# ScalarE in place of VectorE for the absolute values of ten FP4 weight blocks, with other delays in the order of a decoder kernel

## The chip, the core and the metric

The kernel runs on one core of one Trainium2 chip. The metric is the device time of one execution, in microseconds (us). The engines are called as in the profile: PE (TensorE matmuls), PEld (TensorE weight loads), DVE (VectorE), ACT (ScalarE), POOL (GpSimd) and SP (SyncE, which here only issues DMAs).

## The reference

The input is 16 sequences of 128 tokens with 256 features, a context of the same shape and an integer mask. Two layers follow each other, each of self-attention, cross-attention and a feed-forward part, each part followed by a residual sum and a layer norm:

- layer 0 attention: 16 heads, queries and keys projected to 32 latent features with a rotary table, causal softmax;
- layer 0 cross-attention: linear attention with the context (`q (k^T v)`), an affine layer norm;
- layer 0 feed-forward: a gated unit of 704 hidden features, whose three weights and two activations are rounded to FP4;
- layer 1 attention: causal softmax and a second, linear term (`leaky_relu`, `sigmoid`);
- layer 1 cross-attention: masked softmax, and within it a feed-forward part of 1024 hidden features;
- layer 1 feed-forward: one linear map, weights and activations rounded to FP6.

The part that the change touches is this rounding, along the last dimension in blocks of 16:

```python
scale = jnp.maximum(jnp.max(jnp.abs(xb), axis=-1, keepdims=True) / 6.0, 1e-12)
xn = xb / scale
idx = jnp.searchsorted(_MID, jnp.abs(xn))
q = _GRID[idx] * jnp.sign(xn) * scale
```

with the grid 0, 0.5, 1, 1.5, 2, 3, 4, 6 and the midpoints between its values. Everything is float32.

## The kernel before

**Work and stages.** A tile is one sequence: 128 tokens on the partitions. `stages(b, s)` is the work of sequence `b` from the first projection to the output DMA. It is a Python generator, as are its parts (`l0_attn`, `l0_xattn`, `l0_ffn`, `l1_attn`, `l1_xattn`, `l1_ffn`) and the helpers in them. Eight sequences are in flight, each in a place of its own in SBUF (`place0` to `place7`, tags `A`, `B`, `C`, `D`, `x`, `v` with the number of the place); when one ends, another starts in its place. Sequences 0 to 7 are the first wave, 8 to 15 the second.

**The order.** Nothing is scheduled by the compiler. A generator yields what its next step needs: an engine, buffers, tiles that must have been written. A class `Clock` keeps at build time an estimate of when each engine is free and when each tile is written; `Run.start()` gives from it the time at which a step could begin. The loop at the end of `decoder_kernel` looks at all generators, takes those that could begin within 0.05 us of the earliest, and among them first one that holds an open tile, then the one whose time of readiness plus a delay, rounded to steps of 2 us, is the earliest. The delays are the 17 numbers of `DELAY`: one for each sequence (the weights share the first) and one for `fold_values`, which prepares layer 0's value weights. That step's instructions are then issued on their engines; each engine runs its own instructions in the order of issue, waiting on semaphores. So one changed estimate or delay moves what comes after on all engines. Nearly all instructions bear line 208, which is the recording helper's.

**Fillers.** `Timed.fill` (line 147) is called before each step that begins on PE. Where the estimate has PE idle for at least `LEAST` us, it issues small bf16 matmuls into a spare PSUM bank (`ps_filler`, line 161) for 75% of the gap. They compute nothing that is used.

**Weights.** `quantised_weights` is a generator like the others. It takes `w_gate` and `w_up` in three blocks each of 128x512 (in buffers that the profile calls `raw_e`, `raw_A`, `raw_B` for the gate and `raw_C`, `raw_D`, `raw_t` for the other), and `w_down` in four of 128x384 or 128x320 (`raw_down`); rounds each with `fp4`; transposes it on PE (`ps_wt_...`) and copies it with ACT to `gu` and `down`. The first wave's feed-forward (`ps_pg`, `ps_pu`, then `ps_tr_hq` and, after a copy `hT`, `ps_dn`) waits for these. The buffers that hold the raw blocks lie in the eighth place, which sequence 7 takes when the weights are done.

**Rounding.** `to_grid` makes on DVE the block maximum `am`, the scale `sc` and its reciprocal `rc`; the product with `rc`; then the step of the grid at each value from its absolute value, in `st` (tiles `fc_...`); then rounds by adding and subtracting it, and multiplies with `sc`. The absolute value has two ways in FP4, by the parameter `by_act`, which is False in all calls:

```python
        elif by_act:
            yield "S", xn, sc, st
            S.activation(st, xn, AF.Abs)
            yield "V", st, xn, sc
        else:
            yield "V", xn, sc, st
            V.tensor_scalar(st.bitcast(U32), xn.bitcast(U32), 0x7FFFFFFF, None, ALU.bitwise_and)
```

In the second way the pass over the bits stands on DVE; FP6 (`low is None`) uses ACT already.

**Attention.** Scores are written to one PSUM tile of four banks, `quad`, of which there is one: scores `ps_s`, row maxima on DVE (`nm`), their three bf16 terms on POOL (`maxima`), a transpose `ps_tm`, the scores again transposed `ps_st` with the maxima subtracted, exponentials on ACT (`e`), for causal attention a select on POOL, products with the values `ps_yp`, a copy `ys`, transposes `ps_ty`, the division on DVE. Names that end in `_a` are the self-attentions, in `_x` the cross-attention of layer 1. `ps_lat` is the latent projection of layer 0 (with `rope` on DVE).

Of the kernel before, what the change touches and what calls it, by code (L numbers as in the profile page):

```python
# [15 lines left out]
B, T, D, H, HD, LAT = 16, 128, 256, 16, 16, 32  # L16
# [5 lines left out]
NFC = 6  # L22
HID = 1024
EPS = 1e-5
SHARE, LEAST = 0.75, 1.4

DELAY = (0.04, 0.26, 0.15, 0.27, 0.15, 0.52, 0.34, 0.45, 0.56, 0.30, 0.28, 0.08, 0.47, 0.04, 0.22, 0.10, 0.51)
WINDOW = 3.413


# [183 lines left out]
def decoder_kernel(ctx: ExitStack, tc: tile.TileContext, a: dict, out: bass.AP):  # L214
# [31 lines left out]
    def mine(s, tag, shape, name, dtype=F32):  # L246

        return ring(own, f"{tag}{s}", 1, shape, dtype, name)
# [34 lines left out]
    def arrives(t):  # L283
        clock.wrote[clock.key(t)] = ("Q", max(clock.free["PE"], clock.free["Q"]) + 2.5)
# [19 lines left out]
    for g in range(4):  # L304
        n = 512 if g < 3 else NB
# [62 lines left out]
    for i in range(0, 5, 2):  # L368
        n = min(2, 5 - i)
# [68 lines left out]
    def bank(shape, name, dtype=F32):  # L438
        return psum(ps_p, "p", shape, name, dtype)

    def work(tag, bufs, shape, name, dtype=F32):
        return ring(wk, tag, bufs, shape, dtype, name)
# [24 lines left out]
    g, c, n = place["a1p"]  # L467
# [47 lines left out]
    def transposed(src, n_chunks, dst, name):  # L515

        yield "PE", "p", src
        t = bank((n_chunks, P), f"tr_{name}")
        for i in range(n_chunks):
            PE.transpose(t[:, i, :], src[:, i * P : (i + 1) * P], ident)  # L520
        yield "S", t
        S.copy(dst, t)
# [171 lines left out]
    def to_grid(dst, src, n, size, top, least, magic, low, name, by_act=False):  # L694

        width = n * size  # L700
        lock = "fC" if width > D else "fc"
        yield "V", lock, src
        st = work(lock, 1, [P, width], f"fc_{name}")
        s3 = src.rearrange("p (n s) -> p n s", s=size)
        am, sc, rc = (ring(sm, k + lock, 1, [P, n], F32, f"{k}_{name}") for k in ("am", "sc", "rc"))
        V.tensor_reduce(am, s3, AX.X, ALU.max, apply_absolute_value=True)
        V.tensor_scalar(sc, am, 1.0 / top, least, ALU.mult, ALU.max)
        V.reciprocal(rc, sc)
        if low is not None:
            V.tensor_scalar(rc, rc, low, None, ALU.mult)  # L710
        yield "V", rc, sc, st
        xn = dst
        x3 = xn.rearrange("p (n s) -> p n s", s=size)
        V.tensor_tensor(x3, s3, rc.unsqueeze(2).to_broadcast([P, n, size]), ALU.mult)
        if low is None:

            yield "S", xn, st, sc
            S.activation(st, xn, AF.Abs)
            yield "V", st, sc
            V.scalar_tensor_tensor(xn, st, -(2.0**-23), xn, ALU.mult, ALU.add)  # L720
# [7 lines that stand above are left out]
        V.tensor_scalar(st, st, 1.5, magic, ALU.max, ALU.mult)  # L728
        yield "V", xn, st, sc
        V.tensor_tensor(xn, xn, st, ALU.add)  # L730
        V.tensor_tensor(xn, xn, st, ALU.subtract)
        yield "V", xn, sc, st
        V.tensor_tensor(
            dst.rearrange("p (n s) -> p n s", s=size), x3, sc.unsqueeze(2).to_broadcast([P, n, size]), ALU.mult
        )

    def fp4(dst, src, width, name, by_act=False):

        yield from to_grid(dst, src, width // 16, 16, 6.0, 1e-12, 2.0**22, 1.0 - 2.0**-23, name, by_act)

    def fp6(dst, src, width, name):

        yield from to_grid(dst, src, width // 32, 32, 7.5, 1e-30, 2.0**20, None, name)
# [185 lines left out]
    def quantised_weights():  # L929
        yield ("V",)  # L930
        GP.memset(down[:64, NFC - 1, :], 0.0)
        downs = []
        for which, name in enumerate(("w_gate", "w_up")):
            for t, i, j in raws[name]:
                q = t[:, i : i + 2, :].rearrange("p j d -> p (j d)")
                yield from fp4(q, q, 2 * D, f"{name}_{j}")
                yield "PE", "p"
                p = bank((4, P), f"wt_{name}_{j}")
                for jj in range(2):
                    for kc in range(2):  # L940
                        PE.transpose(p[:, 2 * kc + jj, :], q[:, jj * D + kc * P : jj * D + (kc + 1) * P], ident)
                n = min(2 * P, FF - j * P)
                clock.kept.discard(clock.key(t))
                yield "S", p
                for kc in range(2):
                    S.copy(
                        gu[:, which, kc, j * P : j * P + n],
                        p[:, 2 * kc : 2 * kc + 2, :].rearrange("p j n -> p (j n)")[:, :n],
                    )
            for at, n in ((0, 384), (384, 320)):  # L950
                q = mine(NS - 1, "ABCD"[len(downs)], [P, n], f"raw_down_{which}_{at}")
                nc.sync.dma_start(out=q, in_=a["w_down"][:, which, at : at + n])
                downs.append((which, at // P, n, q))
        for j, f0, n, q in downs:
            yield from fp4(q, q, n, f"down_{j}_{f0}")
            yield "PE", "p"
            t = bank((3, P), f"wt_down_{j}_{f0}")
            for f in range(3):
                at = min(f * P, n - P)
                PE.transpose(t[:, f, :], q[:, at : at + P], ident)  # L960
            yield "S", t
            if f0 == 0:
                S.copy(down[:, 0:3, j * P : (j + 1) * P], t)
            else:
                S.copy(down[:, 3:5, j * P : (j + 1) * P], t[:, 0:2, :])
                S.copy(down[64:, 5, j * P : (j + 1) * P], t[64:, 2, :])
        release("gu", [gu, down])
        release("place", [gu])
        for j in range(2):
            yield "V", "t2"  # L970
            q = work("t2", 3, [P, D], f"raw_f1_{j}")
            nc.sync.dma_start(out=q, in_=a["w_f1"][:, j, :])
            arrives(q)
            yield "V", q
            yield from fp6(q, q, D, f"wf1_{j}")
            yield from transposed(q, 2, wf[:, :, j * P : (j + 1) * P], f"wf1_{j}")
# [221 lines left out]
    def release(name, tiles):  # L1198
        if name == "place":
            name = f"place{NS - 1}"  # L1200
        at = max(clock.done(t) for t in tiles)
        free[name].extend([at] * (B if name in ("gu", "wv", "bt") else 1))
# [47 lines left out]
    for name in ("w_x1v", "w_x1o", "w_1", "w_2"):  # L1250
        load(name, nc.sync)
    runs = [
        Run(-1, NS, fold_values(), ("PE",)), Run(0.7, NS, later_biases(), ("PE",)),
        Run(0.5, NS, quantised_weights(), ("V",)),
    ]
    opened.clear()
# [17 lines left out]
    while runs:  # L1274
        able = [(r.start(), r.age, r) for r in runs]
        able = [r for r in able if r[0] is not None]
        first = min(r[0] for r in able)


        at, _, run = min(  # L1280
            (r for r in able if r[0] <= first + 0.05),
            key=lambda r: (not r[2].held, round((r[2].ready + DELAY[int(r[1]) if r[1] >= 0 else B]) / 2.0), r[1]),
        )
        run.step(at)
        if run.need is None:
            runs.remove(run)
# [116 lines left out]
```

## Time and profile before

| | us |
|---|---|
| median of 3 runs | 964.27 |
| lowest, highest | 961.06, 965.34 |
| profiled execution | 960.91 |
| its span, first to last instruction | 959.2 |

| engine | busy, us | share of the span |
|---|---|---|
| PE | 891.0 | 93% |
| DVE | 701.0 | 73% |
| ACT | 515.7 | 54% |
| POOL | 432.5 | 45% |

DMA moves 25.6 MB, mostly in the first 72 us. PE's clock is granted at 0.99 of full speed in the mean. A line of a group reads: line, engine, operation, output and inputs, shapes, count, then busy us and mean ns of one, then the idle time of the engine just before these instructions and what ended it. A wait reads: engine and tile that waited, engine and tile that it waited for, us in total, times, longest. Matmuls overlap in the array, so the means of single matmuls add up to more than PE's busy time.

### The profile page before, as it was taken

What the parts mean: (1) busy time and instruction counts of PE and PEld (TensorE: products, weight loads), DVE (VectorE), ACT (ScalarE), POOL (GpSimd) and SP (SyncE); (2) the same over time, 40 slices, a digit from 0 to 9 for tenths busy, and PEclk for the clock granted to TensorE, in tenths of its full rate; (3) what the DMA queues carried; (4) which work ended last, traced back from release to release, by engine and by line L of the source; (5) the groups of instructions that cost most, each with busy time, mean ns of one, the idle gap of its engine ahead of it and who ended that gap; (6) DMA issues with size and microseconds to landing.
All of it is one profiled execution on the core that took longest, in us unless ns stands there. A gap on an engine that the chain in (4) does not pass through costs nothing.

```text
span 959.2 us, 28184 instructions
## 1 busy us (share of the span) xinstructions
PE 891.0 (93%) x11882; PEld 711.3 (74%) x11882; DVE 701.0 (73%) x1440; ACT 515.7 (54%) x1119; POOL 432.5 (45%) x898
## 2 busy tenths in 40 slices
PE   6788999899999999999999999998999999999985
PEld 6575666676878788878887776776777878877863
DVE  5899999778975945554768788759858687654564
ACT  3254374475577555555455456546765664654532
POOL 3325444465444446343444454554435353453332
PEclk9999999999999999999999999999999999999998
DMA  7920100000000000010000000000000000100000
GB/s 232 207 71 7 29 13 2 15 10 10 11 23 5 12 27 20 18 30 13 13 15 27 23 25 23 13 13 11 15 10 7 16 6 2 37 5 24 2 12 11
DMA packets 47863, 25.55 MB, mean 27 GB/s; under 512 B 23005, under 2 KB 45517, under 8 KB 47481
## 3 DMA queue, kind: packets, MB, share of 16 engines
q1 hardware_dynamic: 46816, 22.39, 8.6%
q8 instruction: 93, 1.52, 0.6%
q0 software_dynamic: 192, 0.93, 0.4%
q10 hardware_dynamic: 728, 0.44, 0.2%
q14 instruction: 34, 0.27, 0.1%
HBM read 19.57 MB, written 2.10 MB: 23 GB/s over the span
## 4 chain that ended last, share of the span: by engine, by line
PE 53%; DVE 30%; ACT 6%; POOL 6%; issue 4%; POOLq 0%; ACTq 0%; DVEq 0%
PE ps_ff L208 10%; PE ps_s_a L208 3%; DVE nm_a L208 3%; PE ps_st_a L208 3%; DVE rope L208 3%; PE ps_a1qk L208 2%; DVE hh L208 2%; PE ps_st_x L208 2%; PE ps_qk L208 2%; PE ps_dn L208 2%; PE ps_pg L208 2%; PE ps_yt L208 2%; PE ps_pu L208 2%; PE ps_yp_a L208 2%; PE ps_s_x L208 2%
## 5 line engine op out<-in xcount | busy, mean ns | idle before, releaser
L208 POOL TENSOR_SCALAR_AFFINE_SELECT e_a<-e_a 128x1024 f32<-128x1024 f32 x64 | 78.4, 1227 | 75.4 <-ACT e_a L208 75.2
L208 DVE TENSOR_REDUCE nm_a<-ps_s_a 128x16 f32<-128x2048 f32 x32 | 73.1, 2283 | 17.3 <-PE ps_s_a L208 17.2
L208 ACT ACTIVATE e_a<-ps_st_a 128x1024 f32<-128x1024 f32 x64 | 65.7, 1032 | 17.7 <-PE ps_st_a L208 17.5
L208 ACT ACT_TABLE_LOAD x47 | 60.3, 1283 | 12.7 <-DMA brow<-in_rows_dram 8.8
L208 PE MATMUL ps_ff<-yT_x1t,w 128*128 128x128 f32 x512 | 62.9, 276 | 0.5 <-ACT yT_x1t L208 0.5
L208 PEld LDWEIGHTS ps_ff<-yT_x1t,w 128*128 128x128 f32 x512 | 60.1, 192 | 2.4 <-issue 0.9
L208 PE MATMUL ps_ff<-w,ff 128*128 128x256 f32 x256 | 61.3, 383 | 0.0
L208 PEld LDWEIGHTS ps_ff<-w,ff 128*128 128x128 f32 x256 | 46.3, 190 | 7.6 <-issue 1.8
L208 ACT ACTIVATE ff<-ps_ff,cols 128x128 f32<-128x128 f32 x128 | 36.6, 370 | 27.4 <-PE ps_ff L208 27.0
L208 POOL CAST maxima<-nm_a 128x16 bf16<-128x16 f32 x32 | 9.8, 307 | 89.1 <-DVE nm_a L208 89.1
L208 PE MATMUL ps_dn<-qw_down,hT 128*128 128x256 f32 x192 | 47.5, 384 | 1.1 <-ACT yT_x1t L208 1.1
L208 DVE TENSOR_REDUCE nm_x<-ps_s_x 128x16 f32<-128x2048 f32 x16 | 36.5, 2282 | 11.4 <-PE ps_s_x L208 11.4
L208 PE MATMUL ps_pg<-gu,yT_xq 128*128 128x352 f32 x128 | 44.1, 467 | 0.1
L208 PE MATMUL ps_pu<-gu,yT_xq 128*128 128x352 f32 x128 | 43.1, 459 | 0.0
L208 ACT ACTIVATE x_x<-z_x,rstd_x 128x256 f32<-128x256 f32 x32 | 19.2, 601 | 42.5 <-POOL rstd_x L208 39.2
L208 PEld LDWEIGHTS ps_dn<-qw_down,hT 128*128 128x128 f32 x192 | 34.6, 190 | 8.0 <-issue 2.1
L208 ACT ACTIVATE e_x<-ps_st_x 128x1024 f32<-128x1024 f32 x32 | 31.5, 1023 | 15.7 <-PE ps_st_x L208 15.7
L208 ACT ACTIVATE x_a<-h_a,rstd_a 128x256 f32<-128x256 f32 x32 | 19.3, 603 | 31.8 <-POOL rstd_a L208 30.6
L208 PE MATMUL ps_yp_a<-e_a,v_a 128*32 128x128 f32 x1024 | 35.3, 276 | 1.1 <-POOL e_a L208 1.1
L208 POOL TENSOR_TENSOR rot<-rope,rope 128x512 f32<-128x512 f32 x16 | 21.3, 1330 | 29.6 <-DVE rope L208 27.8
L208 PEld LDWEIGHTS ps_pu<-gu,yT_xq 128*128 128x128 f32 x128 | 24.3, 190 | 13.5
L208 POOL TENSOR_TENSOR x1k<-x1k,mb 128x512 f32<-128x512 f32 x16 | 21.8, 1365 | 27.2 <-ACT x1k L208 27.2
(367 smaller groups left out, 2638.0 us busy)
## 6 DMA issues: line engine op xcount, KB each, us to landing
ctx<-in_ctxT_dram SPq DMA_DIRECT2D x32, 128.0 KB
xT_in<-in_xT_dram SPq DMA_DIRECT2D x16, 128.0 KB
w<-in_w_dram SPq DMA_DIRECT2D x2, 1024.0 KB
x_in<-in_x_dram SPq DMA_DIRECT2D x16, 128.0 KB
out_dram<-out SPq DMA_DIRECT2D x16, 128.0 KB
a1qa<-x_f SPq DMA_DIRECT2D x16, 127.0 KB
mi<-in_mask_dram SPq DMA_DIRECT2D x16, 64.0 KB
rows<-in_rows_dram POOLq DMA_DIRECT2D x1, 768.0 KB, 5.7
```

The lines of the kernel that those rows point to most:

```text
L208: return f(*args, **kw)
```

## The change

The FP4 rounding of the ten weight blocks takes its absolute values with an ACT activation (`AF.Abs`) in place of DVE's pass over the bits; the rounding of activations stays as it was. The 17 delays are others, `LEAST` goes from 1.4 to 1.2 us, and the loop takes only entries that could begin at the earliest time, where it allowed 0.05 us more.

```diff
-SHARE, LEAST = 0.75, 1.4
+SHARE, LEAST = 0.75, 1.2
-DELAY = (0.04, 0.26, 0.15, 0.27, 0.15, 0.52, 0.34, 0.45, 0.56, 0.30, 0.28, 0.08, 0.47, 0.04, 0.22, 0.10, 0.51)
+DELAY = (0.04, 0.25, 0.07, 0.45, 0.31, 0.03, 0.03, 0.44, 0.09, 0.44, 0.38, 0.30, 0.51, 0.36, 0.34, 0.24, 0.46)
...
-                yield from fp4(q, q, 2 * D, f"{name}_{j}")
+                yield from fp4(q, q, 2 * D, f"{name}_{j}", True)
...
-            yield from fp4(q, q, n, f"down_{j}_{f0}")
+            yield from fp4(q, q, n, f"down_{j}_{f0}", True)
...
-            (r for r in able if r[0] <= first + 0.05),
+            (r for r in able if r[0] <= first + 0.0),
```

## The prediction

> **What bounds the kernel now.** I read the page first: the busy shares and the forty slices.
>
> ```profile
> span 959.2 us, 28184 instructions
> PE 891.0 (93%) x11882; PEld 711.3 (74%) x11882; DVE 701.0 (73%) x1440; ACT 515.7 (54%) x1119; POOL 432.5 (45%) x898
> ...
> PE   6788999899999999999999999998999999999985
> ...
> DVE  5899999778975945554768788759858687654564
> ...
> PEclk9999999999999999999999999999999999999998
> ...
> PE 53%; DVE 30%; ACT 6%; POOL 6%; issue 4%; POOLq 0%; ACTq 0%; DVEq 0%
> ```
>
> One slice is 24 us. PE is full from slice 7 on. In slices 2 to 6 it is DVE that is full, and PE is not. The last line is the chain that ended last: ACT holds 6% of it. The busy time of each engine in three stretches (after the length: PE, PEld, DVE, ACT, POOL; near the end the granted clock) says the same in numbers:
>
> ```profile
> 24.00:144.00 120.00, 103.62 (x1496) 73.35 (x1496) 114.27 (x212) 53.49 (x110) 50.66 (x82) 0.98 0.28 65
> 144.00:912.00 768.00, 739.12 (x9970) 598.34 (x9972) 546.91 (x1119) 438.75 (x948) 358.22 (x747) 1.00 0.05 15
> 912.00:959.00 47.00, 33.04 (x271) 24.84 (x263) 25.95 (x71) 15.27 (x38) 13.99 (x36) 0.94 0.04 12
> ```
>
> From 24 to 144 DVE is busy 114.3 of 120 us, while PE has 16.4 us free and spends 11 of its 103.6 on filler. From 144 to 912 PE is idle 28.9 of 768 us. In the last 47 us it is idle 14. So an edit can save DVE time at the beginning, PE idle time spread thinly over the middle, or idle time in the tail. The chain at 39 to 46 us shows the removed pass on the path:
>
> ```profile
> 39.49 0.61 DVE raw_B L208
> ...
> 40.13 1.43 DVE fc_w_gate L208
> ...
> 41.58 0.44 DVE fc_w_gate L208
> ...
> 43.46 2.21 DVE nm_a L208
> ```
>
> **Removed and added passes.** DVE loses ten passes over the bits. The groups by form give them: four of 0.427, 0.417, 0.426 and 0.428 and one more of 0.427 us, one of 1.421 (raw_B, while GpSimd ran a tensor_tensor), two of 0.338 and two of 0.588: 5.40 us in all. ACT gains ten Abs. No 128x512 Abs is in the trace; bounds are the 128x256 Abs of fp6 and the 128x512 Identity with a pointer bias:
>
> ```profile
> L208 ACT ACTIVATE fc_f<-f1q 128x256 f32<-128x256 f32 x16 | 6.7, 417 | 1.9 <-DVE f1q L208 1.9
> ...
> L208 ACT ACTIVATE q<-ps_qfk,wqk_b 128x512 f32<-128x512 f32 x16 | 11.1, 692 | 4.2 <-PE ps_qfk L208 4.1 <-DMA w_x1o<-in_w_x1o_dram 0.2
> L208 DVE TENSOR_SCALAR fc_w_gate<-raw_B 128x512 uint32<-128x512 uint32 x1 | 1.4, 1421 | 0.0
> ```
>
> I take 0.61 us, from 0.417 plus 256 elements at 0.73 ns (the slope from the 0.370 us of a 128x128 ACTIVATE to the 1.023 of a 128x1024 one), and 0.51 for 384 columns. That adds some 5.8 us to ACT, which has more than half of 24 to 144 free. What matters is whether DVE waits for the answer. The built order of the changed kernel shows what stands between the product and the next pass on DVE. For six blocks there is other work: raw_A (the l2o sum, and its wait for PE), raw_C (a 2.28 us maximum), raw_t (0.67 us) and three of the four down blocks (over 1 us each). There the pass is saved whole: 0.417 + 0.426 + 0.427 + 0.588 + 0.338 + 0.588 = 2.78 us. For four blocks nothing stands between, and DVE waits for Abs with 0.05 us of hand-over: raw_e 0.66 for 0.427, +0.23; raw_B 0.66 for 1.421, -0.76; raw_D 0.66 for 0.428 and about 0.5 behind an exponential that ACT has queued ahead, +0.73; the first down block 0.56 for 0.338, +0.22. Sum: -2.78 + 0.42 = **-2.4 us** on a stretch that DVE bounds. Bounds: -5.4 (no wait shows) to +4: Abs stands in ACT's order behind an exponential once and once behind the copy of ys, which itself waits for PE; that copy's chain (exponential 1.03, select 1.23, products 1.0, copy 0.59) is 3.9 us if none of it is done. Behind the waiting DVE pass are rope and the score maxima, for which PE waits.
>
> The Trainium skill speaks against this move: "ScalarE: Activation LUTs", section "Rules for kernel authors", sends simple elementwise operations to VectorE and not to ScalarE. The rows agree on the durations (0.396 us on DVE against 0.417 on ACT at 256 columns, both SBUF to SBUF); by the rule alone the term would be a small loss, ten times 0.02, and the sum below -2.7 in place of -5.3. The rule does not ask which engine is full, and from 24 to 144 us it is DVE.
>
> **The order.** The delays, the choice among ready entries (0.05 us became 0.0) and LEAST reorder everything. Four things can be read from the built order.
>
> Table loads fall from 47 to 35, as silu and exponentials alternate less often; no Abs brings one. ACT's timeline shows a load's price:
>
> ```profile
> 203.49 1.28 ACT L208 ACT_TABLE_LOAD   x1
> 204.78 0.47 ACT L208 ACTIVATE silu<-ps_pg 128x352 f32<-128x352 f32 x1
> 205.27 1.28 ACT L208 ACT_TABLE_LOAD   x1
> 206.56 1.02 ACT L208 ACTIVATE e_a<-ps_st_a 128x1024 f32<-128x1024 f32 x1
> ```
>
> So 12 x 1.283 = 15.4 us less on ACT. ACT has 6% of the chain: **-0.9 us**, bounds 0 to -15.4. "ScalarE: Activation LUTs", section "What ACT_TABLE_LOAD costs", adds a drain of about 1.38 us to each load, which would make 12 x 2.66 = 31.9 and -1.9 on the path; here a load begins 0.02 us after the instruction before it and the next begins 0.01 after it, so no drain is seen.
>
> The tail. From the end of the last masked scores (918.5) to the first feed-forward product of batch 15 (933.7) pass 15.2 us, in which PE has 11.5 us of work by its own rows. Waits of PE from 912 on:
>
> ```profile
> PE ps_tr_f L208 <- DVE f1q L208: 2.9, 2, 1.9
> PE ps_tr_x1t L208 <- DVE x L208: 2.7, 2, 1.6
> PE ps_tr_x1y L208 <- DVE y_x L208: 1.0, 1, 1.0
> ```
>
> In the changed order three batches end together: 17.8 us of PE work stand in that place, enough to cover the chain of batch 15, and one more output projection (1.2 us) has moved behind its last product, into time in which PE only fills. I take **-4 us**: the 3.7 idle, the 1.2, less about 1 for a new planned gap ahead of batch 14. Bounds -7 to +1.
>
> Fillers go from 99 to 111 (47 to 66 before the first down product, 16 to 7 in the middle, 36 to 38 at the end). At 23.0 us for 99 that is 2.8 us, and 4.4 for the 19 at the beginning. They are set where PE is planned idle, and DVE covers them: **0**, bounds 0 to +4.4.
>
> The down product. It needs the copy of the transposed activations (0.35 to 0.62 us on ACT). In the old order at least 1.8 us of PE work stands between in 15 of 16 batches. In the new one eight have 0.3, 0.4, 0.4, 0.5, 0.9, 1.1, 1.2 and 1.3. With a copy that starts at once (0.7 us) they lack 1.2 us together; with the shortest time that the old trace shows (1.73) 7.7. I take **+2**.
>
> The rest of the order is the unknown. By 48 us slices PE's time without work varied by about 1.7 us from slice to slice in the middle, so 16 slices of another order differ by some 7, and two orders by 10: **0**, bounds -10 to +10.
>
> Sum: -2.4 - 0.9 - 4 + 0 + 2 = -5.3 us. The profiled execution took 960.91 (span 959.2 and 1.7 around it), 3.4 under the median of the runs; on it the sum gives 955.6, and on the median of 964.27 it gives **959.0**. About 0.5%, 4.8 us, is what a measurement here can tell from no change, so the forecast lies just beyond it. Its own range is 950 to 963.
>
> **Rivals.** One: the order takes back what the edit and the tail give (chance 0.25). For it: PE's planned gaps, by the fillers, are about as long as before, and the middle has only 28.9 us of idle to win. Then the time is 964, between 959.5 and 969.
>
> Two, slower (0.32): the copies for the down product come late. Place: eight down products between about 145 and 600 us. If the copy finds ACT in a pair of exponentials (2 x 1.03), each lacks 0.7 + 2.06 us less its cover, together 8 x 2.76 - 6.1 = 16 us in place of the 2 counted: -7.3 + 16 = +8.7, 973 us. It decides from 12.1 us, 1.5 for each product. Against it: ACT is free 45% of the time, and loses 12 loads.
>
> That the change does not do what it says is ruled out by the built order: ten DVE passes are gone, ten Abs are on ACT, nothing else in the counts but loads and fillers differs.
>
> **The numbers.** Faster (0.43) holds the forecast and larger gains, for which the bounds of loads and order leave room to 945. The low end, 946, takes in the order's -10 on the forecast; the high end, 975, takes in rival two.
>
> **What would show it.** Right: DVE busy near 109 of 24 to 144 and the first down product earlier than 145.7 us; no wait of PE for the last batch's x over 1 us; 35 loads. Wrong: DVE idle on fc for over 4 us in all; PE waiting for yT or hT before ps_dn by over 5 us; PE idle over 35 us from 144 to 912.

## The result and the profile after

| | before | after |
|---|---|---|
| median, us (9 runs each, side by side) | 962.35 | 970.11 |
| lowest to highest | 960.88 to 965.34 | 965.74 to 975.63 |
| profiled execution, its span | 960.91, 959.2 | 972.47, 970.8 |

The ratio is 1.0084, with a 95% interval of 1.0061 to 1.0108: the changed kernel is **slower by 0.84%**, 7.8 us. The forecast was 959.0, faster. Its range (946 to 975) holds the result; its direction was wrong. Three runs below were far longer than the others of their kernels (1033 us in `abs_old_order`, 1032 us in `old_order_pads`, 3026 us in the kernel before beside the last four experiments) and are left out of all medians, clocks and ratios.

First the page of the changed kernel, the same lines as before.

```profile
span 970.8 us, 28196 instructions
PE 902.8 (93%) x11891; PEld 717.6 (74%) x11894; DVE 686.6 (71%) x1430; ACT 503.7 (52%) x1117; POOL 431.8 (44%) x898
...
PE   6889889899999899999999999999999999999996
...
DVE  4977989876994736476576788995678575674645
...
PEclk9998999999999999999999999999999999999998
...
PE 57%; DVE 24%; ACT 6%; POOL 5%; issue 4%; SPq 3%; DMA 2%; ACTq 0%; POOLq 0%; DVEq 0%
```

Read span and PE together. The span has grown by 11.6 us (959.2 to 970.8) and PE's busy time by 11.8 (891.0 to 902.8), with twelve more fillers (111 after 99) and nothing else added to PE; a few matmul records are missing from this trace. So PE is idle for as long as before, 68.0 us against 68.2. In these two executions the loss is no idle time at all: PE is *busy* longer with the same work. DVE was relieved (701.0 to 686.6, its share of the chain from 30 to 24%). Of these 14.4 us the ten passes are 5.4; most of the rest comes with the order (`bits_new_order` below keeps the passes and has 692.8). PE's share of the chain went up from 53 to 57%. In the clock's row the fourth slice has an 8.

The three stretches of the prediction (columns: start and end, length, then PE, PEld, DVE, ACT, POOL busy, granted clock, DMA share, GB/s):

```profile
24.00:144.00 120.00, 102.92 (x1442) 72.43 (x1442) 101.94 (x194) 51.87 (x111) 49.65 (x78) 0.94 0.27 64
144.00:912.00 768.00, 736.91 (x9904) 594.53 (x9904) 541.09 (x1117) 424.34 (x934) 355.82 (x746) 0.99 0.05 15
912.00:959.00 47.00, 42.15 (x374) 33.83 (x375) 27.93 (x76) 17.60 (x47) 14.64 (x34) 0.97 0.02 7
```

From 24 to 144 us DVE is busy 12.3 us less than before, and PE's idle time does not follow: 17.1 us against 16.4. What did change is the clock, 0.94 after 0.98. Cut at the places where the granted clock changes, it looks like this:

```profile
65.70:69.10 3.40, 1.68 (x28) 1.05 (x16) 3.23 (x8) 2.08 (x5) 1.09 (x1) 1.00 0.18 48
69.10:72.50 3.40, 2.78 (x42) 2.27 (x46) 3.23 (x5) 1.50 (x3) 1.16 (x1) 0.51 0.02 5
72.50:75.90 3.40, 3.40 (x51) 2.52 (x48) 0.33 (x1) 1.77 (x3) 1.09 (x1) 0.50 0.00 0
86.20:89.60 3.40, 1.49 (x11) 0.99 (x10) 3.35 (x9) 1.61 (x5) 1.29 (x4) 1.00 0.00 0
89.60:93.00 3.40, 3.33 (x9) 2.49 (x9) 1.70 (x5) 0.76 (x2) 1.77 (x3) 0.50 0.00 0
127.20:130.60 3.40, 1.63 (x12) 1.09 (x11) 3.19 (x8) 2.52 (x7) 1.64 (x2) 1.00 0.00 0
130.60:134.00 3.40, 3.40 (x8) 1.87 (x6) 3.16 (x9) 3.35 (x5) 1.14 (x1) 0.50 0.00 0
659.70:663.10 3.40, 1.49 (x36) 0.95 (x30) 1.94 (x4) 1.22 (x2) 2.92 (x5) 1.00 0.00 0
663.10:666.50 3.40, 3.40 (x21) 2.01 (x15) 0.00 (x0) 1.80 (x3) 2.25 (x3) 0.50 0.00 0
```

The rows come in pairs. In the first of each, PE is busy for less than half of a stretch of 3.4 us, because it waits. In the next stretch the clock is granted at half, and PE is busy nearly all of it. (The two rows after 69.10 are both at half.) PE's timeline shows the work itself taking twice as long (start, us, then what):

```profile
66.94 0.66 PE L208 MATMUL ps_ty_a<-ident,ys_a 128*128 128x128 f32 x4
69.53 0.66 PE L208 MATMUL ps_tr_a<-ident,y_a 128*128 128x128 f32 x2 [1.93 <-DVE y_a L208]
...
73.15 1.94 PE L208 MATMUL ps_yp_a<-e_a,v_a 128*32 128x128 f32 x32
```

PE waits 1.93 us for `y_a`, and four us later 32 products with the values take 1.94 us that take 1.08 elsewhere. Over 60 to 670 us the changed kernel has seven such half-clock stretches, where the kernel before has two. In the kernel before's trace the stretches at half clock with work in them are at 21.9, 93.6, 656.8 and 878.7 us; these are the last two pairs, where the second follows 2.05 us of busy time:

```profile
653.40:656.80 3.40, 1.21 (x8) 0.68 (x7) 3.19 (x7) 3.37 (x6) 0.68 (x1) 1.00 0.19 54
656.80:660.20 3.40, 3.40 (x32) 3.12 (x30) 3.37 (x6) 1.85 (x5) 1.59 (x2) 0.50 0.03 9
875.30:878.70 3.40, 2.05 (x55) 1.74 (x55) 0.49 (x3) 1.77 (x3) 1.30 (x2) 1.00 0.20 54
878.70:882.10 3.40, 3.40 (x45) 2.69 (x39) 0.00 (x0) 2.18 (x3) 0.00 (x0) 0.50 0.02 5
```

A stretch costs half of the time that PE is busy in it, up to 1.7 us. Added up over all stretches at half clock, PE lost 6.6 us to it before and **15.0 us** after. Twelve fillers at 0.22 us are another 2.7. The two are 11.1 of the 11.6 us. This says where the time lies in two executions, not yet what put it there.

The Trainium skill's "TensorE: Matmul & The Clock Gate", section "What's actually happening", has the two states and a free-running window of 3413 ns, in which activity is counted; the rows agree with both. In "HAM oscillation — how this bites in real kernels" it gives as an abstract rule that gaps of PE should not exceed some 3.4 us. Here that is not enough: the longest single waits ahead of these stretches are 1.3 to 1.9 us, and what counts is the sum of idle time in one window (before 130.6 us the longest wait is 1.3 us, and PE is busy for only 1.63 of 3.40). As the window runs free of the kernel, a wait may or may not fall into one window as a whole, so times should vary with the clock from run to run. They do: the changed kernel's nine runs go from 965.74 us at a mean clock of 0.989 to 975.63 at 0.979, though not in strict order (974.21 at 0.984).

### The profile page after: what moved, and what is told of

The parts are those of the page before. It is cut to its first block, busy times and chain, and to the rows that moved or that the text cites. A ratio compares the mean times of both kernels' runs of the same rounds, so it can differ in the third digit from the quotient of the medians.

```text
span 970.8 us, 28196 instructions
## 1 busy us (share of the span) xinstructions
PE 902.8 (93%) x11891; PEld 717.6 (74%) x11894; DVE 686.6 (71%) x1430; ACT 503.7 (52%) x1117; POOL 431.8 (44%) x898
## 4 chain that ended last, share of the span: by engine, by line
PE 57%; DVE 24%; ACT 6%; POOL 5%; issue 4%; SPq 3%; DMA 2%; ACTq 0%; POOLq 0%; DVEq 0%
PE ps_ff L208 8%; PE ps_s_a L208 3%; PE ps_pg L208 3%; PE ps_st_a L208 3%; PE ps_a1qk L208 3%; PE ps_pu L208 3%; PE ps_op_a L208 3%; DVE hh L208 2%; DVE rope L208 2%; PE ps_dn L208 2%; PE ps_qk L208 2%; DVE nm_a L208 2%; PE ps_st_x L208 2%; PE ps_yp_a L208 2%; PE ps_x0kv L208 2%
## 5 line engine op out<-in xcount | busy, mean ns | idle before, releaser
L208 POOL TENSOR_SCALAR_AFFINE_SELECT e_a<-e_a 128x1024 f32<-128x1024 f32 x64 | 75.0, 1173 | 76.3 <-ACT e_a L208 71.7
L208 DVE TENSOR_REDUCE nm_a<-ps_s_a 128x16 f32<-128x2048 f32 x32 | 73.1, 2285 | 14.3 <-PE ps_s_a L208 14.2
L208 PE MATMUL ps_pg<-gu,yT_xq 128*128 128x352 f32 x128 | 46.7, 489 | 0.5 <-ACT yT_xq L208 0.5
L208 POOL TENSOR_SCALAR_AFFINE_SELECT maT<-maT 128x1024 f32<-128x1024 f32 x16 | 18.4, 1149 | 45.6 <-ACT maT L208 45.6
L208 PEld LDWEIGHTS ps_yp_a<-e_a,v_a 128*32 128x32 f32 x1024 | 26.6, 112 | 11.0 <-POOL e_a L208 3.9
L208 PE MATMUL ps_qk<-xT_in,w_qkv 128*128 128x128 f32 x256 | 34.2, 295 | 0.2 <-DMA xT_in<-in_xT_dram 0.2
```

Source lines behind the costliest of these rows:

```text
L208: return f(*args, **kw)
```

## The experiments

**How they were made.** In most of these kernels the order is not planned but replayed. The loop that chooses is replaced by the written-out list of its 2890 choices (2880 for the kernel before), one letter for each step of a generator. So an edit can be made in an unchanged order, and an order without the edit. Fillers are planned with the `LEAST` of the order that is used, and anew for each order, so their number differs.

```diff
+STEPS = ("zzaazwwwwaaaww...", ...)
-    while runs:
-        able = [(r.start(), r.age, r) for r in runs]
...
+    for c in STEPS:
+        run = next(r for r in runs if r.age == ages[c])
```

**What was measured.** Ratios stand against the kernel before, run beside each on the same chip. The clock of the kernel before is the mean of the 20 runs beside the first four experiments. "Idle" is span less PE's busy time from the profiled run's page; "half clock" is half of PE's busy time in the stretches granted at half; "fillers" counts 0.22 us each, those set by hand included. The last column is what is left of PE's busy time: the useful work at full clock.

| kernel | median, us | ratio (95%) | mean clock of its runs | idle | half clock | fillers | useful |
|---|---|---|---|---|---|---|---|
| before | 962.35 | 1 | 0.989 | 68.2 | 6.6 | 21.6 | 862.8 |
| after | 970.11 | 1.0084 (1.0061 to 1.0108) | 0.984 | 68.0 | 15.0 | 24.3 | 863.5 |
| abs_old_order | 963.23 | 1.0020 (1.0006 to 1.0035) | 0.988 | 71.1 | 6.8 | 21.6 | 862.0 |
| bits_new_order | 972.0 | 1.0099 (1.0072 to 1.0126) | 0.983 | 67.6 | 14.7 | 24.3 | 863.0 |
| old_start_new_rest | 967.81 | 1.0064 (1.0042 to 1.0087) | 0.988 | 68.3 | 4.9 | 23.2 | 865.4 |
| new_start_old_rest | 972.18 | 1.0095 (1.0065 to 1.0125) | 0.986 | 71.9 | 13.5 | 26.4 | 861.5 |
| new_order_pads | 971.54 | 1.0104 (1.0082 to 1.0126) | 0.991 | 63.9 | 5.1 | 35.0 | 864.4 |
| new_scores_late | 972.4 | 1.0122 (1.0085 to 1.016) | 0.981 | 72.0 | 16.9 | 21.0 | 863.2 |
| old_order_new_tail | 973.17 | 1.0126 (1.0105 to 1.0147) | 0.986 | 70.2 | 8.5 | 26.0 | 866.9 |
| abs_replanned | 1004.78 | 1.0451 (1.0426 to 1.0476) | 0.973 | 83.7 | 26.9 | 28.2 | 865.5 |
| new_order_pads2 | 965.05 | 1.0028 (1.0014 to 1.0043) | 0.992 | 61.1 | 6.2 | 32.8 | 863.8 |
| bits_new_pads2 | 965.11 | 1.0035 (1.0021 to 1.0049) | 0.993 | 60.6 | 6.8 | 32.8 | 863.5 |
| old_order_no_fillers | 968.09 | 1.0068 (1.0044 to 1.0093) | 0.972 | 85.3 | 25.2 | 0 | 860.2 |
| old_order_pads | 961.82 | 1.0003 (0.9986 to 1.0019) | 0.989 | 68.0 | 9.2 | 25.1 | 861.9 |

The last column is 860 to 867 in all fourteen. So idle time, fillers and half clock make up the differences of span to within some 4 us; less than that cannot be read from this table. Its last four columns are of one profiled execution each, which can lie off the median: it was the fastest of nine for `old_start_new_rest` (963.57 us), and the longest of six for `new_start_old_rest` (974.99) and `old_order_no_fillers` (972.37).

### The edit and the order apart

The edit in the old order (`abs_old_order`). As the order is kept step by step, DVE waits for each Abs with nothing in between:

```diff
         elif by_act:
-            yield "S", xn, sc, st
-            S.activation(st, xn, AF.Abs)
-            yield "V", st, xn, sc
+            yield "V", xn, sc, st
+            clock.run("V", st, [xn], V._cost("tensor_scalar", st, [xn])[0])
+            nc.scalar.activation(st, xn, AF.Abs)
...
-                yield from fp4(q, q, 2 * D, f"{name}_{j}")
+                yield from fp4(q, q, 2 * D, f"{name}_{j}", True)
```

> The steps are issued in the old kernel's order, written out as a list, with its fillers; only the ten absolute values of the weights are taken by ACT instead of DVE, and DVE's next pass follows at once, so that DVE waits for each of the ten. If the hand-over from DVE to ACT and back is what makes the changed kernel slower, this one is slower than the old by several us too, towards +8 us. If the new order is the cause, the ten waits cost 0.66 us each for 0.54 saved, and the time stays within 2 us of the old kernel's.

Measured: 963.23 us, slower by 0.2%. DVE's waits from 24 to 150 us (waiting tile, awaited tile, sum, times, longest):

```profile
DVE fc_w_up L239 <- ACT fc_w_up L755: 5.7, 3, 4.2
DVE fc_down L239 <- ACT fc_down L755: 1.3, 2, 1.1
DVE fc_w_gate L239 <- ACT fc_w_gate L755: 1.1, 2, 0.7
```

DVE waits 8.1 us to save passes of 5.4 us; once 4.2 us for an Abs of 0.65, which ACT has queued behind passes that wait for PE's projections. That is 2.7 us more waiting than passes saved, and the kernel lost 2.2 us by the medians.

The order without the edit (`bits_new_order`): the changed kernel's 2890 steps, in which ACT's step is only accounted for and DVE makes the pass over the bits.

```diff
         elif by_act:
             yield "S", xn, sc, st
-            S.activation(st, xn, AF.Abs)
+            clock.run("S", st, [xn], S._cost("activation", st, [xn])[0])
+            nc.vector.tensor_scalar(st.bitcast(U32), xn.bitcast(U32), 0x7FFFFFFF, None, ALU.bitwise_and)
             yield "V", st, xn, sc
```

> The steps in the changed kernel's order, written out as a list, with its fillers; only the ten absolute values are DVE's pass over the bits again, at the same place in DVE's order. If the order is the cause, it stays slower than the old kernel by 6 to 10 us (0.6 to 1.0%). If the hand-over is the cause, it is back within 2 us of the old kernel. By the sum of the prediction, which gave Abs 2.4 us of gain, it is 2.4 us slower than the changed kernel.

Measured: 972.0 us, 1.0099 (1.0072 to 1.0126, beside 1.0061 to 1.0108 for the whole change). The new order alone is slower by as much as the whole change. The edit is not the cause.

### Which part of the order

`old_start_new_rest` takes the first 500 of the new order's steps in the old order's sequence and the rest from the new one; `new_start_old_rest` is the reverse. Both keep DVE's bits. In words:

```diff
+STEPS = first 500 steps of one order, in the sequence of the other, then the rest of the one
```

> The passes over the bits stay on DVE. The first 500 of 2890 steps of the changed order (to about 180 us) are put into the order that they have among each other in the old kernel; the rest is the changed order. If the loss is made in the start, where DVE and the weights hold PE up, it goes: within 3 us of the old kernel, or below it by the tail's 3 us. If it is made in the order of the middle, 5 to 9 us remain.

> The reverse: the passes over the bits on DVE, the first 500 of 2890 steps of the old order put into the order that they have in the changed kernel, then the old order. If the loss is made in the start, this one is slower than the old kernel by 6 to 10 us. If it is made in the middle, it is within 3 us of the old kernel.

Measured: 967.81 and 972.18 us; both halves lose. PE does the same products in every kernel, so the traces can be laid over each other by PE work done (each product weighted with its usual distance to the next one in the trace of before, 826 us in all). How much later than before a kernel reaches a point, in us:

| PE work done (time before) | after | bits_new_order | old_start_new_rest | new_start_old_rest |
|---|---|---|---|---|
| 40 (63) | +2.0 | +2.1 | 0.0 | +3.8 |
| 60 (90) | +6.0 | +6.5 | +1.3 | +6.9 |
| 140 (190) | +8.5 | +9.3 | +2.7 | +13.6 |
| 300 (366) | +12.5 | +13.3 | +6.9 | +13.7 |
| 500 (578) | +16.0 | +17.1 | +8.9 | +13.7 |
| 600 (691) | +13.9 | +13.3 | +4.4 | +13.7 |
| 700 (798) | +13.8 | +13.2 | +5.5 | +13.7 |

The changed kernel and its order without the edit lose in the same places to within 1.1 us. (The figures move by 1 to 2 us with the weights chosen.) Up to 190 us they lose 8.5 and 9.3, mostly where the half-clock stretches are. From there to 578 us the new order loses 6 to 8 more with and without the new start, and then gains a part back; `new_start_old_rest`, once in the old order, loses nothing more. That middle part is mostly idle time: over the same work PE is idle 10.6 us before (190 to 578 us) and 16.8 after (190 to 594), with 1.7 us lost at half clock beside it. The rows from 320 to 620 us, before and after:

```profile
320.00:620.00 300.00, 291.38 (x4165) 237.76 (x4153) 209.12 (x436) 164.18 (x365) 141.60 (x291) 1.00 0.07 20
```

```profile
320.00:620.00 300.00, 287.33 (x4043) 235.60 (x4041) 206.23 (x432) 152.87 (x357) 139.46 (x289) 0.99 0.07 20
```

PE is idle 8.6 us before and 12.7 after; the longest waits after are of 1.6 to 2 us (for `y_a`, `rope` and `a1k`), and `old_start_new_rest` shows them too. That kernel's column above is of its fastest run. By the medians it loses some 6 us, at nearly the mean clock of before (0.988 beside 0.989). `new_start_old_rest` loses some 9 us, of which its clock (0.986) makes about 3 and its 22 extra fillers up to 5. So the new order loses in two ways: behind the start mostly by waits, and at the start by the clock and the fillers (in the changed kernel's trace half clock makes 6.7 of the 8.5 us up to 190).

### Is it the clock, or the waits ahead of it?

A stretch at half clock follows a wait. To part the two, useless matmuls are put into the waits: they shorten no wait and add work to PE, but keep the clock. First attempt, `new_order_pads`:

```diff
+PADS = dict(tr_a0_0=6, v0_3=6, op_a0_2=3, tr_xq_0=5, tr_a0_3=4, ty_a0_6=5, tr_x1a_0=6, tr_f1_1=6, pg_12_0=8)
         t = ring(pool, tag, 4, [P, 512], F32, "ps_" + name)
+        for _ in range(PADS.get(name, 0)):
+            nc.tensor.matmul(t, lhsT=ident_b, rhs=ones3.unsqueeze(1).to_broadcast([P, 4, P]), start=True, stop=True)
```

> The new order with ScalarE's Abs, step by step as in the changed kernel, but with 49 short filler matmuls (bf16, 128x512, about 0.22 us each) put by hand ahead of nine PE instructions that wait in its trace: transposes tr_a0_0 (6), tr_xq_0 (5), tr_a0_3 (4), tr_x1a_0 (6), tr_f1_1 (6), ty_a0_6 (5), value product v0_3 (6), output product op_a0_2 (3), up/gate product pg_12_0 (8). They do 10.8 us of useless work, inside waits that last 1.0 to 2.5 us each. Theory 'clock' (a 3.41 us stretch in which PE was busy for under half is followed by one at half clock, and seven of these stretches between 60 and 670 us are most of the loss): at most two of the seven are left, the mean granted clock rises from about 0.984 to 0.988 or more, and the time falls by 5 to 10 us, to 960 to 965. Theory 'waits' (the order makes PE wait for DVE and ACT, and the half clock lies where PE would wait anyhow): the clock rises all the same, but the time stays within 2 us of the changed kernel's 970, or is up to 3 us worse by fillers that do not end in time.

Measured: 971.54 us, no gain, though the clock went up to 0.991. That is what "waits" expected, but the timeline shows another reason:

```profile
85.76 0.55 PE L240 MATMUL ps_wt_down<-ident,raw_down 128*128 128x128 f32 x3 [0.36 <-DVE raw_down L240]
87.94 1.45 PE L459 MATMUL ps_v<-ones,ident_b 128*128 128x512 bf16 x6 [1.63 <-DVE bd L240]
89.23 0.28 PE L240 MATMUL ps_v<-bl,sel 128*128 128x272 bf16 x1
```

The six fillers (line 459) stand behind the wait of 1.63 us, not in it: PE waits there for the bank into which they write (their operands are constants), and then does 1.3 us of nothing. One more group of six stood so, and around three others (17 fillers) no wait was left to fill. In the profiled runs half clock fell by 9.9 us (15.0 to 5.1), but of the 10.7 us of fillers only 4.1 came out of idle time (68.0 to 63.9); the span was 2.4 us shorter, and the median not at all. The run does not part the two theories.

So the second attempt, `new_order_pads2`, with 39 fillers only where the bank is free, or one product earlier; and the same with DVE's bits, `bits_new_pads2`.

```diff
-PADS = dict(tr_a0_0=6, v0_3=6, op_a0_2=3, tr_xq_0=5, tr_a0_3=4, ty_a0_6=5, tr_x1a_0=6, tr_f1_1=6, pg_12_0=8)
+PADS = dict(tr_a0_0=6, wt_down_0_0=5, tr_xq_0=5, tr_a0_3=4, ty_a0_6=6, ff2_2=5, yp_a0_14=8)
```

> As in the first kernel with fillers by hand (new order, ScalarE's Abs), but each group of short matmuls now stands ahead of an instruction whose bank is free while PE waits for an operand, or one product earlier where the wait was for the bank: tr_a0_0 (6), wt_down_0_0 (5), tr_xq_0 (5), tr_a0_3 (4), ty_a0_6 (6), ff2_2 (5), yp_a0_14 (8); 39 matmuls, 8.5 us. There the fillers took away the half clock (PE's work lost to it 15.0 us in the changed kernel's trace, 5.1 with them), but 23 to 29 of the 49 stood behind the wait and cost their own time. Theory 'clock' (the profiled loss of 11.6 us is 8.4 us of half clock and 2.7 us of more fillers, with PE's idle time the same 68 us): most of the 8.5 us falls into idle time, and the time is 960 to 966 at a clock of 0.988 or more. Theory 'waits': 968 to 973, whatever the clock.

> The same order and the same 39 fillers, with VectorE's bits in place of ScalarE's Abs: the edit by itself where the clock disturbs it less. The forecast's term was -2.4 us for Abs in the new order: then this kernel is 1.5 to 4 us slower than the one with Abs. If Abs gains nothing there (the time saved on DVE ends in another wait of PE): within 1 us of it.

Measured: 965.05 us, 1.0028 (1.0014 to 1.0043). The interval lies clear of the changed kernel's (1.0061 to 1.0108). Eight and a half us of useless work made it **5 us faster**. PE's timeline at the place shown above, and the page:

```profile
70.67 0.66 PE L240 MATMUL ps_ty_a<-ident,ys_a 128*128 128x128 f32 x4
71.16 1.46 PE L459 MATMUL ps_tr_a<-ones,ident_b 128*128 128x512 bf16 x6
73.16 0.44 PE L240 MATMUL ps_tr_a<-ident,y_a 128*128 128x128 f32 x2 [0.55 <-DVE y_a L240]
...
75.60 1.08 PE L240 MATMUL ps_yp_a<-e_a,v_a 128*32 128x128 f32 x32
```

```profile
span 963.9 us, 28273 instructions
...
PE 902.8 (94%) x11933; PEld 716.6 (74%) x11933; DVE 687.5 (71%) x1430; ACT 504.4 (52%) x1117; POOL 432.1 (45%) x898
```

PE still waits for `y_a`, but six fillers stand in most of that time; the products with the values take 1.08 us again. PE is busy 902.8 us, as in the changed kernel: the fillers have replaced the 8.8 us lost to half clock (15.0 less 6.2), and the span is shorter by the idle time that they filled (68.0 to 61.1). The clock theory holds for the larger part. What is left, 0.28%, no run takes apart.

`bits_new_pads2` took 965.11 us. With a steadier clock the edit is worth 0.06 us by the medians and 0.5 us by the means of these twelve runs each, on one chip (95% interval -0.8 to 1.7). The forecast's 2.4 lies outside.

The reverse test, `old_order_no_fillers`: the old order, fillers planned but not issued.

```diff
             c.run("PE", bank, (), cost, 0.17)
-            self._e.matmul(bank, lhsT=lhsT, rhs=rhs, start=True, stop=True)
```

> VectorE's bits and the old order with all 99 fillers left out, nothing else moved: it does 21.6 us less of useless PE work. Theory 'clock': PE is under half busy in more stretches of 3.41 us, each followed by one at half clock, 5 or more beyond the kernel before's in the first 150 us; each costs up to 1.7 us: 966 to 980, clock below 0.982. Theory 'waits' (the clock falls where PE waits anyhow): 957 to 963, though the clock falls.

```profile
span 970.7 us, 27983 instructions
...
PE 885.4 (91%) x11783; PEld 714.6 (74%) x11783; DVE 699.7 (72%) x1440; ACT 516.4 (53%) x1119; POOL 432.1 (45%) x898
...
PEclk9879799999999899989999999999999999999997
```

Measured: 968.09 us, 1.0068. With 21.6 us of work taken away PE's busy time falls by only 5.6 in the profiled run (the longest of the six), because 18.6 us more are lost to half clock (25.2 after 6.6). That is the size that the clock can have in this kernel, with no step moved.

`old_order_pads` put 16 fillers into three waits of the old order, the dict being `ty_a0_2=5, ty_a0_14=7, tr_x1t_12=4`.

> VectorE's bits and the old order with 16 more fillers ahead of ty_a0_2 (5), ty_a0_14 (7) and tr_x1t_12 (4), where the profiled run of the kernel before falls to half clock (93.6, 656.8 and 878.7 us). Theory 'clock': two or three of these stretches go, 1.7 us each: 956 to 959 beside 961, clock 0.992 or more. Theory 'waits': 960 to 963.

Measured: 961.82 us, 1.0003 (0.9986 to 1.0019), no gain. The three stretches were gone in its profiled run, but others fell to half clock (25, 28, 72 and 923 us). In the old order few are left, and fillers set by one run's trace do not catch the next one's.

### Three more orders

`new_scores_late` moves five steps of sequence 2 (its scores up to the copy of the transposed maxima) behind the first exponentials of sequences 0 and 1. In the changed kernel DVE waits 3.9 us for these scores, where PE first does 7.4 us of projections for sequences 3 to 6. The steps in short form, not in code (the number is the sequence; `tm`, `mT`, `ST`, `e`, `sel` are the steps named under "Attention", `mxGP` the three terms on POOL):

```diff
-... 0:tm 2:SCORES 0:mT 1:tm 2:nm 1:mT 0:ST 2:mxGP 2:tm 0:e0 0:sel0 2:mT ... 0:sel1 ...
+... 0:tm 0:mT 1:tm 1:mT 0:ST 0:e0 0:sel0 ... 0:sel1 2:SCORES ... 2:nm ... 2:mxGP ... 2:tm ... 2:mT ...
```

> The new order with ScalarE's Abs; only the five steps of sequence 2 from its scores to the copy of the transposed maxima are moved behind the first exponentials of sequences 0 and 1, so that DVE meets sequence 2's score maximum eight passes later. Theory 'start' (in the stretch that DVE bounds, DVE waits 3.9 us for sequence 2's scores and passes that wait on to everything after it): that wait is under 1 us, the last transposes of the weights and the first down product come 3 us or more earlier than in the changed kernel (122 and 167 us there), and the time is 965 to 967. Theory 'clock': the half-clock stretches after 66 us stay where they are, and the time stays at 968 to 972. If the wait only moves to the next pass of DVE, the same.

Measured: 972.4 us. The wait did not go, it changed its place and grew. DVE's waits, and ACT's timeline:

```profile
DVE fc_w_up L239 <- ACT fc_w_up L239: 7.8, 1, 7.8
```

```profile
57.51 1.14 ACT L239 ACTIVATE qk<-ps_qk,cols 128x128 f32<-128x128 f32 x4 [0.65 <-PE ps_qk L239]
...
60.14 1.02 ACT L239 ACTIVATE e_a<-ps_st_a 128x1024 f32<-128x1024 f32 x1 [0.62 <-PE ps_st_a L239]
61.06 0.62 ACT L239 ACTIVATE fc_w_up<-raw_D 128x512 f32<-128x512 f32 x1
```

The Abs of `raw_D`, 0.62 us long, stands in ACT's queue behind the passes that take those same projections out of PSUM and behind an exponential; DVE, which has its product ready at 53.9, waits 7.8 us for it. An Abs that waits for nothing itself still waits for all that ACT has queued ahead.

`old_order_new_tail`: the old order for the first 2600 steps, then the new one.

> VectorE's bits and the old order for the first 2600 of 2890 steps, then the new order for what is left (from about 860 us on). The forecast counted -4 us for the tail alone, with bounds of -7 to +1. If that was right: 956 to 959 beside about 961 for the kernel before, and PE waits under 1 us for the last batch's x. If the tail's gain in the changed kernel only gave back what it had lost before: 960 to 963.

Measured: 973.17 us, slower. The seam costs more than the tail can give: PE waits 4.4 us for `nm_x` and 3.0 for `mb` around it.

```profile
PE ps_st_a L239 <- DVE nm_x L239: 4.4, 1, 4.4
PE ps_tr_x1t L239 <- DVE mb L239: 3.0, 1, 3.0
```

Laid over the trace of before, it is 13.8 us late at 750 us of PE work and 12.4 at the end: behind the seam the new tail gains 1.4 us. As a test of the tail's whole term it is not clean.

`abs_replanned` has only the edit: the old delays, `LEAST` and 0.05 us, and the planner free to make its order from the changed costs.

```diff
-                yield from fp4(q, q, 2 * D, f"{name}_{j}")
+                yield from fp4(q, q, 2 * D, f"{name}_{j}", True)
...
-            yield from fp4(q, q, n, f"down_{j}_{f0}")
+            yield from fp4(q, q, n, f"down_{j}_{f0}", True)
```

> Only ScalarE's Abs on the ten blocks; the delays, the choice among ready entries and the least gap for fillers stay as before, and the planner makes another order of its own from the changed costs. Theory 'this order' (the new delays made an order that is bad at the start): 958 to 964. Theory 'any order' (the order before was the best of many, and any other of the planner's loses by its waits): 966 to 974, with most of the loss before 250 us and a granted clock below 0.987.

```profile
span 1004.3 us, 28252 instructions
...
PE 920.6 (92%) x11910; PEld 726.1 (72%) x11912; DVE 686.1 (68%) x1430; ACT 511.9 (51%) x1123; POOL 437.0 (44%) x898
...
PEclk9889999999999999999999999999999999999968
```

Measured: 1004.78 us, slower by 4.5%, far outside what either theory gave. Idle time is up by 15.5 us and half clock by 20.3; part of both lies at the end, where the last batch is left alone (from 912 us on PE is idle for 18.8 us, where it was 14.2 before, at a mean clock of 0.88). So a kernel with the same ten Abs is slower by 0.2% in the old order, by 4.5% in the order that the old delays make of the changed costs, and by 0.84% in the one of the new delays. The spread is the order's.

## Why the prediction was wrong, by its steps

**What failed: "the rest of the order", 0 with bounds of 10 us.** `bits_new_order`, which has the order without the edit, is slower by 0.99%, 9.5 us (6.9 to 12.1). The sum had all of the order's terms at -2.9 (loads, tail, fillers, down product and this one). The bounds were worked out from PE's *idle* time from slice to slice, with PE's busy time taken as fixed. What grew was busy time, 8.4 us at half clock and 2.7 us of fillers in the profiled run, while idle time, of which the forecast meant to save some 5 us, stayed (68.0 us after 68.2): the tail gained 3.0, but the middle lost 6.2 (190 to 578 us). Over the medians the clock's part is smaller: mean clocks of 0.984 and 0.989 make at most 4.8 of the 7.8 us (15.3 of 968 us less 10.5 of 960); with the fillers' 2.7 that is nearly all of it. The evidence was in the trace of before: 0.98 and 0.94 stood in two of the three rows that the prediction quoted, and the 99 fillers were there for a reason that it did not ask for.

**Abs, -2.4: too much.** The passes were sized well (0.63 us forecast as 0.61; DVE waited 2.8 us for ACT's `fc` tiles of the weights, where the forecast's four uncovered blocks make about 3.0). What failed was "on a stretch that DVE bounds". DVE was busy 12.3 us less from 24 to 144 us (5.0 of it the nine removed passes that lie there; nine other instructions now fall outside), and PE's idle time did not fall. Other waits came in DVE's own queue:

```profile
DVE h_a L208 <- PE ps_op_a L208: 5.9, 2, 3.8
DVE nm_a L208 <- PE ps_s_a L208: 3.9, 1, 3.9
```

Before, the longest of DVE's waits in that stretch was 1.1 us. A high busy share over 120 us did not mean that each DVE pass in them lay on the path. The worth measured is 0.5 us (-0.8 to 1.7) in the new order with the second set of hand-set fillers, and a loss of 2.2 us in the old order.

**Tail, -4: right in kind, smaller.** No wait for the last batch's `x` exceeds 1.0 us, as forecast:

```profile
PE ps_ty_x L208 <- ACT ys_x L208: 1.5, 1, 1.5
PE ps_tr_f L208 <- DVE f1q L208: 1.3, 1, 1.3
PE ps_tr_x1t L208 <- DVE x L208: 1.0, 1, 1.0
```

From 912 us to the end PE is idle 11.2 us, 14.2 before. By the work done the changed kernel gains 2.3 us behind 798 us, with a half-clock stretch at 956.6 in it. So the term is -3 in idle time and -2.3 in all.

**Fillers, 0.** They were counted as covered by DVE. Their price is small, but their use was overlooked: they hold the clock.

**Down product, +2, and rival two.** PE waits 1.0 us for `hT` from 144 to 912 us, in three waits. The mechanism of rival two was not there.

**Table loads, -0.9.** 35, as forecast. No run isolates their worth.

**Rivals.** By its number rival two was nearest (+8.7 us beside the measured +7.8), but by luck, as its mechanism was not there. By its mechanism rival one (the order takes the gains back) was nearest; it set the loss at 0.

Of the signs named, "DVE idle on fc for over 4 us", "PE waiting before ps_dn by over 5 us" and "PE idle over 35 us from 144 to 912" (it was 31.1) all stayed on the side of "right", while the kernel became slower. DVE was busy 101.9 of 24 to 144 where 109 was named, which looked better still and meant waiting. The first down product came at 167.5 us, not before 145.7: the one sign that told of the loss.

What stays open: which of the new delays makes which wait. `LEAST` and the choice among ready entries were not changed alone either. The waits of the middle part are located, but none was taken away by itself.

## What to carry to other kernels

Set span against PE's idle *and* busy time before and after; where busy time grows with equal work, look for stretches at half clock, and for waits that leave PE under half busy in the 3.4 us ahead of each. In these runs useless matmuls paid where their bank was free while PE waited, and cost their full time where they needed the bank that PE waited for. Where a planner makes the order, replay the old order with the edit and the new order without it: that showed in two runs that 0.84% belonged to the order.

## What the runs showed of the hardware

- Waits of 1.3 to 1.9 us can cost 1.7 us more, up to four us later, on matmuls that wait for nothing: PE busy for 1.5 to 1.7 of 3.40 us, then 3.4 us at a clock of 0.50.
- How sharp this is, counted over all fourteen profiled runs from 20 us on, in the steps of 3.41 us in which the clock changes. Of 84 steps at full clock with PE busy for under half (1.71 us), 74 were followed by half clock, among them all 41 with under 1.4 us. Of 3692 steps with more, 10 were, none with over 2.26 us. So the limit is near half, but not exactly half of what the records call busy.
- Ahead of 20 us it is otherwise: in nine of the fourteen runs the clock fell at 13.6 to 15.3 us after a step with PE busy for 2.6 to 3.4 us (in the changed kernel at 14.5). No run shows why.
- The mean clock differs between runs of one kernel, so the half-clock stretches do too. Over the nine runs of the changed kernel (0.979 to 0.989) the time rises by about 1 us for each 0.001 of mean clock that is lost.
- Taking 99 useless matmuls out of the old order made it 0.68% slower.
